# Pacing SyncE's transfers by steps of VectorE, and copying a first product ahead of the exponentials, in a one-core transformer block

## The chip, the cores and the metric

The kernel runs on one core of a Trainium2 chip. The metric is the device time in microseconds (us) of one execution; lower is better. The core has five engines, each with its own queue of instructions that it runs in order: TensorE (PE; PEld is its loading of weights), VectorE (DVE), ScalarE (ACT), GpSimd (POOL) and SyncE (SP). SyncE issues all transfers here; they run on the core's 16 DMA engines. Instructions of different engines wait for each other through semaphores.

## What is computed

16 sequences of 256 tokens with 256 channels go through one block, all in float32:

```
x = x + attention(layernorm(x))      # 16 query heads in 4 groups, 4 key/value heads, 128 wide
x = x + ffn(layernorm(x))            # one 256x256 linear layer, rounded to int8 values
# attention: key s is seen by query t if s <= t and (s < 4 or s >= t - 31)
attn = softmax(q @ k.T / sqrt(128), masked);  out = attn @ v;  return out @ wo.T
# ffn: x and weight are scaled by max|.|/127 per row, rounded, multiplied, scaled back, + bias
```

## The kernel before

**Units and steps.** A unit is one sequence n with one group g of four heads; there are U = 64 units, in the order of `units`. The main loop (`for i in range(U - NT)`) makes 62 steps, one for each of the units 0 to 61; the last two units are written out by hand behind it. Step i computes the scores and the softmax of unit i, the queries of unit i + 1, and parts of the work of older units. Steps 4k to 4k + 3 belong to sequence k.

**Scores.** Queries are taken in blocks of 16 tokens. For each block the keys that it can see (48 in a window and 4 sinks) stand together, so that the scores of a unit are one 128 x 8 x 52 array. `unit_scores` issues TensorE's products into `pss` (L593), VectorE's scaling and masking (L599), the negated row maximum `nmax` (L608), and gives back a function that issues chosen ones of the eight exponentials on ScalarE (L613). `normalised` (L620) divides by the sums, turns the array in 32 x 32 blocks into `z` on VectorE (L627) and stores it as `zd` in DRAM (L629); its inner function `back` reads it again, in four DMAs, as the turned weights `ad` (L638). These `back` functions are kept in `ways[i]`.

**Values.** The values of a sequence are computed for pairs of heads: pair 0 and pair 1. Each takes one chunk of TensorE's work (`start_chunk`; the chunks of sequence n stand at the ends of steps 4n - 3 to 4n, in the order keys 0, values 0, keys 1, values 1). In the step after it, ScalarE copies the products out of PSUM (`both_banks`, L347), GpSimd combines them into `vt`, and `store` writes them as `vd` to DRAM (L536). `values_to` (L457) then reads them into the windows, `vw`: for each half j of the 128 partitions one DMA of 336 KB (L466), one of 16 or 32 KB (L471) and one of 32 KB (L472). There is one `vw` buffer for each pair (`vws`).

**Visits.** In odd steps from 3 on, `times_values` (L675) multiplies the weights `ad` of the units i - 3 and i - 2 with `vw` into `po` (L685). ScalarE copies `po` into `oT` (L696), GpSimd forms sums of it (`left_sums`, L291), and the output projection `py` follows in later steps.

**Queries.** From sequence 1 on, the projections are computed with seven block products in place of eight (Strassen's scheme in Winograd's form). `queries` issues the seven products of two heads into two PSUM banks (`pq`, L89) and returns a `Products`. Its `first` copies the first product to SBUF as `p_q` on ScalarE (L341); `combine` (L326 to L330) makes the two heads' queries `qt` of it in five VectorE operations, whose first one reads that copy. In sequence 0 the products are plain, and one ScalarE copy (L564) takes each over into `qt`. Each step has two such pieces, k = 0 and 1. The pool `ps_m` has four PSUM banks; `pq`, `po`, the chunks' products and others take turns in them.

**What sets the order.** Every engine runs its instructions in the order in which the program writes them (`in_written_order`). Work that belongs to other sequences is hung on a step and a point of it with `at(step, point, f)`, and `do(step, point)` writes it there: loads of x (`load_x`, at "leave" of step 4(n - 1) - 5), statistics (`norm_stats`), the turning of x and of the layer's input through DRAM (`zd_xnT`, `xnT`, `zd_hb`, `hb`; L410 and L419) and the parts of the layer, whose `leave` stores the output. A `back` of an even unit is called at the end of the next step (a visit), that of an odd unit at the start of the step after it; behind the latter, `stores` calls `values_to` for both halves. The lines in question:

```python
        if i - 1 in ways and not visit:
            ways.pop(i - 1)()
            for f in stores:
                f()
            stores = []
...
        for k, q in enumerate(ps):
            exps(range(done, 1 + 3 * k))
            done = 1 + 3 * k
            q.first() if isinstance(q, Products) else q()
        exps(range(done, NK2))
```

So ScalarE's order in a step is: exponential 0, copy for k = 0, exponentials 1 to 3, copy for k = 1, exponentials 4 to 7.

Of the kernel before, what the change touches and what calls it, by code (L numbers as in the profile page):

```python
# [34 lines left out]
def kernel(  # L35
# [11 lines left out]
    nc = tc.nc  # L47
    pe, dve, act, pool, sp = nc.tensor, nc.vector, nc.scalar, nc.gpsimd, nc.sync
    B, T, DM = x.shape
    P = 128  # L50
    D = 128
    H = wqT.shape[1] // D
    G = wkT.shape[1] // D
    HG = H // G
    NC = DM // P
    NT = T // P
# [6 lines left out]
    NJ = 2  # L63
# [33 lines left out]
    def load_x(n):  # L97
        if n < B:
            xts[n] = xp.tile([P, NT, DM], FP, tag="x", name=f"x_{n}")
            sp.dma_start(xts[n], x_v[n])  # L100
# [41 lines left out]
    half = const.tile([P, NT], FP, name="half")  # L142
# [314 lines left out]
    def values_to(n, pair, vd, row):  # L457


        w = vws[pair]  # L460
        vw[n, pair] = w
        base = vd.offset
        for j in range(NJ):
            r = j * HALF
            first = NJ * QB + j * QB - WIN
            sp.dma_start(  # L466
                w[r : r + NW, 1:],
                bass.AP(vd.tensor, base + first * row, [[row, NW], [NJ * QB * row, NK2 - 1], [1, 2 * D]]),
            )
            live = (j + 1) * QB  # L470
            sp.dma_start(w[r + NW - live : r + NW, 0], bass.AP(vd.tensor, base, [[row, live], [1, 2 * D]]))  # L471
            sp.dma_start(  # L472
                w[r + NW : r + NK], bass.AP(vd.tensor, base, [[row, SINK], [0, NK2], [1, 2 * D]])
            )

    def plain_keys(n, pair):
        pk = ps_m.tile([P, 2, T], FP, tag="m", name=f"pk_{n}_{pair}")
# [15 lines left out]
    def plain_values(n):  # L493
        pv = m_banks(f"pv_{n}")
        for t in range(NT):
            for c in range(NC):
                mm(
                    pv[t].rearrange("p k d -> p (k d)"), xnT[n][:, c, t * P : (t + 1) * P], wv_sb[:, c, :],
                    start=(c == 0), stop=(c == NC - 1),
                )  # L500

        def rest():
            vd = dram.tile([T, G * D], FP, tag="vp", name=f"vp_{n}")
            for t in range(NT):
                if t == 0:
                    to = p1.tile([P, 3, 2, D], FP, tag="vt", name=f"vt_{n}_{t}")
                    to = to[:, 0:2].rearrange("p j e d -> p (j e d)")
                else:
                    to = p2.tile([P, HG * T], FP, tag="oT", name=f"vt_{n}_{t}")[:, 0 : G * D]
                act.copy(to, pv[t].rearrange("p k d -> p (k d)"))  # L510
                sp.dma_start(vd[t * P : (t + 1) * P], to)

            def placed(pair):
                values_to(n, pair, vd[:, pair * 2 * D : (pair + 1) * 2 * D], G * D)

            return placed

        return rest
# [9 lines left out]
    def values(n, pair):  # L528
        p = m_banks(f"pv_{n}_{pair}")
        for to, left, right in products(p, factors(n, wv_sb, wv_sums, pair)):  # L530
            mm(to, right, left, start=True, stop=True)
        v = p1.tile([P, 3, 2, D], FP, tag="vt", name=f"vt_{n}_{pair}")

        def store():
            vd = dram.tile([T, 2 * D], FP, tag="vd", name=f"vd_{n}_{pair}")
            sp.dma_start(vd.rearrange("(j p) d -> p j d", p=P), v[:, 0:2].rearrange("p j e d -> p j (e d)"))  # L536
            return lambda: values_to(n, pair, vd, 2 * D)

        return Products(p, f"v_{n}_{pair}", (v[:, 0:3:2, 0], v[:, 2, 1], v[:, 1, 0], v[:, 0:2, 1])), store

# [233 lines left out]
    def by_dma(n):  # L774
        return n < B - 2
# [147 lines left out]
    U = len(units)  # L923
# [2 lines left out]

    POINTS = ("load", "chunk", "gap", "narrow", "early", "turn", "linear", "late", "pool", "leave")
    tasks = {}  # L930

    def at(place, point, f):
        assert point in POINTS
        tasks.setdefault((place, point), []).append(f)

    def do(place, point):
        for f in tasks.pop((place, point), []):
            f()

    chunks = {}  # L940
    for n in range(1, B):
        p = n * G
# [8 lines left out]
    for n in range(2, B):  # L951
        p = (n - 1) * G
        if n > 2:
            at(p - 5, "leave", lambda n=n: load_x(n))
        at(max(p - 4, 1), "early", lambda n=n: norm_stats(n))
        at(p - 2, "early", lambda n=n: norm(n))
        way = []
        at(p - 2, "late", lambda n=n, way=way: way.extend(turned_by_blocks(xns[n], p2, f"xnT_{n}")))
        at(p - 1, "load", lambda way=way: way[0]())
        at(p - 1, "early", lambda n=n, way=way: xnT.__setitem__(n, way[1]()))  # L960
        at(p, "late", lambda n=n: channels(n))
# [10 lines left out]
    for n in range(B - 1):  # L972
        p = n * G + G + 3
        steps = {}

        def step(k, n=n, steps=steps):
            if not steps:
                steps.update(ffn_steps(n))
            steps[k]()

        if by_dma(n):
            plan = (("stats", 1, "early"), ("norm", 2, "early"), ("scale", 2, "late"), ("quantise", 2, "late"),
                    ("clip", 3, "pool"), ("turn", 3, "late"), ("out", 3, "leave"), ("back", 4, "load"),
                    ("narrow", 5, "early"), ("linear", 5, "linear"), ("rest", 7, "early"), ("leave", 8, "leave"))
        else:
            plan = ()
            ffn_last = step
        if n == B - 3:
            ffn_last_but_one = step
            plan = plan[:4]  # L990
        if n == B - 4:
            ffn_last_but_two = step
            plan = plan[:-2]
        for k, after, point in plan:
            at(p + after, point, lambda k=k, step=step: step(k))
# [16 lines left out]
    for f in first_queries:  # L1012
        f()

    ways, waiting, stores, sums = {}, None, [], []
    def start_chunk(i):
        if i == 0:
            return "plain", plain_keys(0, 1)
# [14 lines left out]
    for i in range(U - NT):  # L1033
        visit = i % 2 == 1 and i >= 3
        do(i, "load")
        if i - 1 in ways and not visit:
            ways.pop(i - 1)()
            for f in stores:
                f()
            stores = []  # L1040
        exps, sm = unit_scores(i)
        if i == 0:
            first_values = plain_values(0)
        do(i, "gap")
        kind = waiting and waiting[0]
        if kind == "plain":
            waiting[1]()
        elif kind:
            waiting[3].both_banks()
            waiting[3].combine(pool)  # L1050
        if kind == "v":
            stores.append(waiting[4]())
        for f in sums:
            f()
        sums = []
        do(i, "pool")
        do(i, "turn")
        ps = [queries(*units[i + 1], 0)]
        if i == 0:
            first_values = first_values()  # L1060
            first_values(0)
            at(1, "load", lambda: ways.pop(0)())
            at(1, "load", lambda: first_values(1))
        ps.append(queries(*units[i + 1], 1))
        done = 0
        for k, q in enumerate(ps):
            exps(range(done, 1 + 3 * k))
            done = 1 + 3 * k
            q.first() if isinstance(q, Products) else q()
        exps(range(done, NK2))  # L1070
        for q in ps:
            if isinstance(q, Products):
                q.combine(dve)
        do(i, "early")
        rests = [r for r in (output_part(*o) for o in output_parts(i) if o[0] >= 0) if r]
        for r in rests:
            r[0]()
        values_out = [times_values(u) for u in (i - 3, i - 2)] if visit else []
        for r in rests:
            r[1]()  # L1080
        ways[i] = normalised(i, sm)
        for k, (copied, summed) in enumerate(values_out):
            copied()
            if k == 0:
                summed()
            else:
                sums.append(summed)
        for r in rests:
            r[2]()
        if kind == "k":  # L1090
            keys_to(waiting[1], waiting[2])
        waiting = start_chunk(i)
        if i == U - NT - 1:
            for k in range(2):
                queries(B - 1, G - 1, k, plain=True)()
        do(i, "linear")
        do(i, "late")
        do(i, "leave")
        if i - 1 in ways:
            ways.pop(i - 1)()  # L1100
    assert not tasks and not waiting, sorted(tasks)
    for f in sums:
        f()

    a, b, n = U - 2, U - 1, B - 1
    ways.pop(a - 1)()
    for f in stores:
        f()
    exps_a, sm_a = unit_scores(a)
    exps_b, sm_b = unit_scores(b)  # L1110
    normal_a, turn_a, copied_a = turned_twice(a, sm_a)
# [96 lines left out]
```

## Time and profile before

| what | us |
|---|---|
| three runs | 679.08, 679.09, 682.23 |
| their median | 679.09 |
| the profiled execution | 680.51 |
| its span, first to last instruction | 678.7 |
| DMA packets of queue q1 (SyncE's), MB | 95.34 |
| SyncE's DMAs of values, vw<-vd | 60 of 336 KB, 90 of 32 KB, 30 of 16 KB |
| SyncE's DMAs of weights, ad<-zd | 248 of 64 KB |
| VectorE waiting for the copy p_q (L326 <- L341) | 38.8, in 59 waits |
| ScalarE waiting for nmax (L613 <- L608) | 117.8, in 61 waits |
| VectorE waiting for x (L212) | 13.1, in 10 waits |

Lines of a profile name an engine, a line of the program, an operation and "output<-input" tiles. A row of waits says who waited for whom: total time, number of times, longest. A row of the timeline gives start, duration and, in brackets, how long the engine had been idle before it and what ended that. "Issue" stands for time in which an engine waited for nothing that the profile shows. Windows give the busy time of each engine within a stretch, the granted clock, the mean busy share of the DMA engines and GB/s.

### The profile page before, as it was taken

The numbers are of one execution on the slowest core, as the hardware profiler recorded it, in microseconds if no ns is written. First come the engines' busy times: TensorE is split into PE (matmuls) and PEld (weight loads), VectorE is DVE, ScalarE is ACT, GpSimd is POOL, SyncE is SP. The second block draws the span as 40 slices with busy tenths as digits, with TensorE's granted clock in tenths as the row PEclk, the third lists the DMA queues.
The fourth block names the chain that finished last, engine by engine and source line by source line (L and its number), as shares of the span: only waits on it lengthen the run. The fifth ranks groups of instructions, "written<-read, shape, count | busy, mean of one in ns | idle before, by whom it ended". The sixth has DMA issues, their size and how long they took to land.

```text
span 678.7 us, 35702 instructions
## 1 busy us (share of the span) xinstructions
PE 658.9 (97%) x14956; PEld 623.7 (92%) x14956; DVE 527.0 (78%) x1362; ACT 440.0 (65%) x1626; POOL 527.3 (78%) x823
## 2 busy tenths in 40 slices
PE   9989999999999999999999999999999999999995
PEld 6678899999999999999999999999999999999873
DVE  3757668888788878878788787888869888787775
ACT  3685657657676667667757666766657666665641
POOL 4789578687997868789687887878798787787634
PEclk9999999999999999999999999999999999999998
DMA  8567564566756656666656756556674656656420
GB/s 285 141 169 182 138 146 103 118 163 128 176 138 150 148 117 166 140 155 146 157 130 137 180 139 154 133 118 178 135 178 118 157 140 137 156 128 157 113 67 32
DMA packets 152929, 97.62 MB, mean 144 GB/s; under 512 B 69440, under 2 KB 143040, under 8 KB 152768
## 3 DMA queue, kind: packets, MB, share of 16 engines
q1 hardware_dynamic: 152768, 95.34, 58.4%
q8 instruction: 118, 1.93, 1.3%
q14 instruction: 43, 0.35, 0.2%
HBM read 59.11 MB, written 36.18 MB: 140 GB/s over the span
## 4 chain that ended last, share of the span: by engine, by line
PE 89%; DVE 5%; ACT 2%; issue 2%; DMA 1%; SPq 0%; POOL 0%; DVEq 0%; ACTq 0%
PE py L89 28%; PE pq L89 27%; PE po L685 10%; PE pss L593 8%; PE pk L89 8%; PE pv L89 7%; ACT scores L613 1%; PE pa L89 1%; PE warm L89 1%; DMA vw<-vd 1%; DVE qt L328 0%; ACT qt L564 0%; DVE nmax L608 0%; DVE qt L326 0%; DVE scores L599 0%
## 5 line engine op out<-in xcount | busy, mean ns | idle before, releaser
L613 ACT ACTIVATE scores<-scores,nmax 128x52 f32<-128x52 f32 x512 | 167.9, 332 | 117.8 <-DVE nmax L608 117.8
L89 PE MATMUL pq<-xs,wq_sums 128*64 128x128 f32 x1416 | 122.2, 273 | 0.0
L613 ACT ACTIVATION_READ_ACCUMULATOR scores<-scores,nmax 128x1 f32 x512 | 97.8, 191 | 0.0
L291 POOL TENSOR_TENSOR os<-oT 128x256 f32<-128x256 f32 x56 | 43.8, 781 | 68.8 <-ACT oT L696 68.8
L89 PE MATMUL pq<-xnT,wq_sb 128*64 128x128 f32 (+1 forms) x1104 | 93.9, 290 | 1.5 <-ACT b_v L347 1.5
L89 PEld LDWEIGHTS pq<-xs,wq_sums 128*64 128x64 f32 x1416 | 92.1, 137 | 0.0
L89 PE MATMUL py<-wo_sb,oT 128*64 128x128 f32 (+1 forms) x1152 | 89.7, 297 | 0.0
L696 ACT COPY oT<-po 128x512 f32<-128x512 f32 x124 | 66.4, 588 | 34.5 <-PE po L685 30.5
L685 PEld LDWEIGHTS po<-ad,vw 52*64 52x64 f32 x4096 | 70.8, 134 | 15.8 <-issue 9.6
L89 PE MATMUL py<-wo_sums,os 128*64 128x128 f32 x1344 | 84.6, 273 | 0.0
L685 PE MATMUL po<-ad,vw 52*64 52x64 f32 x4096 | 77.2, 221 | 7.4 <-issue 5.3
L326 DVE TENSOR_TENSOR qt<-pq,p_q 128x256 f32<-128x256 f32 x118 | 49.5, 420 | 38.8 <-ACT p_q L341 38.8
L89 PEld LDWEIGHTS py<-wo_sb,oT 128*64 128x64 f32 x1152 | 70.4, 137 | 8.3 <-issue 0.3
L89 PEld LDWEIGHTS py<-wo_sums,os 128*64 128x64 f32 x1344 | 76.9, 137 | 0.1
L89 PEld LDWEIGHTS pq<-xnT,wq_sb 128*64 128x64 f32 x1104 | 67.6, 137 | 7.3 <-ACT b_v L347 1.7
L593 PE MATMUL pss<-kt,qt 128*64 128x52 f32 x2048 | 72.2, 222 | 0.4 <-ACT qt L564 0.2
L593 PEld LDWEIGHTS pss<-kt,qt 128*64 128x64 f32 x2048 | 70.0, 138 | 2.0 <-ACT qt L564 1.0
L599 DVE SCALAR_TENSOR_TENSOR scores<-pss,masks 128x416 f32<-128x416 f32 x62 | 36.0, 580 | 33.1 <-PE pss L593 33.1
L328 DVE TENSOR_TENSOR qt<-pq,qt 128x256 f32<-128x256 f32 x118 | 50.1, 425 | 13.3 <-PE py L89 0.9
L347 ACT COPY b_v<-pv 128x512 f32<-128x512 f32 (+1 forms) x60 | 31.7, 532 | 42.8 <-PE pv L89 40.7
L89 PE MATMUL pq<-xs,wq_sb 128*64 128x128 f32 x472 | 49.1, 273 | 0.0
L89 PE MATMUL pq<-xnT,wq_sums 128*64 128x128 f32 x472 | 49.1, 273 | 0.0
(192 smaller groups left out, 1622.7 us busy)
## 6 DMA issues: line engine op xcount, KB each, us to landing
vw<-vd SPq DMA_DIRECT2D x60, 336.0 KB
zd<-z SPq DMA_DIRECT2D x62, 256.0 KB
ad<-zd SPq DMA_DIRECT2D x248, 64.0 KB
vd<-vt SPq DMA_DIRECT2D x30, 256.0 KB
x<-in_x_dram SPq DMA_DIRECT2D x15, 256.0 KB
out_dram<-y SPq DMA_DIRECT2D x15, 256.0 KB
zd_xnT<-z_xnT SPq DMA_DIRECT2D x56, 64.0 KB
xnT<-zd_xnT SPq DMA_DIRECT2D x56, 64.0 KB
```

The lines of the kernel that those rows point to most:

```text
L89: pe.matmul(to[c : c + HALF], left[:, c : c + HALF], right, start=start, stop=stop)
L291: pool.tensor_add(s[0], a21, a22)
L326: eng.tensor_add(c11_u, like(p[0][:, 0:2], c11_u), two(p1, c11_u))
L328: eng.tensor_add(c21_c22, like(p[1][:, 0:2], c21_c22), v.unsqueeze(1).to_broadcast(c21_c22.shape))
L347: act.copy(copies[k], self.p[k][:, 0 : 4 - k])
L593: pe.matmul(pss[j * HALF : (j + 1) * HALF, k, :], qt[n, g][:, t, bt].rearrange("p h i -> p (h i)"), kt[n, g // 2][:, g % 2, b, :], start=T ...
L599: dve.scalar_tensor_tensor(s[:, :, 0:NK], pss, SCALE, masks, ALU.mult, ALU.add)
L613: act.activation(s[:, k, 0:NK], s[:, k, 0:NK], AF.Exp, bias=nmax[:, k : k + 1], scale=1.0, accum_out=sm[:, k : k + 1],)
L685: pe.matmul(po[j][d0 : d0 + HALF, k].rearrange("p (a y) -> p a y", a=2), vw[n, g // 2][r, kb, v0 : v0 + HALF], ad[k][r], start=True, stop= ...
L696: act.copy(to[:, j], po[j].rearrange("p k (h i) -> p k h i", i=QB))
```

## The change

`values_to` no longer issues both halves; it returns `half(j)`, which issues the three DMAs of one half. The points of a step are renamed, and three new ones are named after places in VectorE's work. `do_behind(place, point, mark)` writes what hangs on a point and makes the first instruction so written wait for the instruction `mark`, the last one written before: "t2" stands behind `nmax` of the step's scores, "t4" behind the combination of the first queries, "t6" behind that of the second.

- In an even step from 4 on, the weights `ad` of the even unit i - 2 are read at its start, and those of the odd unit i - 1 at "t2".
- Pair 0 of sequence k (combined in step 4k - 1): its first half is read at "t4" of step 4k, its second at "t2" of step 4k + 1. Pair 1 (combined in step 4k + 1): its first half at "t4" of step 4k + 2, its second at "t6" of step 4k + 4.
- `load_x` goes from "leave" to "t6" of the same step, and the output's store from "leave" of one step to "t6" two steps later.
- In ScalarE's order the copy for k = 0 stands ahead of all exponentials, and that for k = 1 behind two of them; the other six follow.

```diff
@@ values_to
-        for j in range(NJ):
+        def half(j):
             r = j * HALF
...
+        return half
@@ values
-            return lambda: values_to(n, pair, vd, 2 * D)
+            return values_to(n, pair, vd, 2 * D)
@@ points
+    written = nc.cur_bb.bb.instructions
+    def do_behind(place, point, mark):
+        k = len(written)
+        do(place, point)
+        if len(written) > k:
+            tc.add_manual_dep(
+                written[k], mark, mybir.DependencyInfo(mybir.DependencyClass.Sync, mybir.DependencyReason.DATA),
+                reason="paced",
+            )
...
-            at(p - 5, "leave", lambda n=n: load_x(n))
+            at(p - 5, "t6", lambda n=n: load_x(n))
...
-                    ("narrow", 5, "early"), ("linear", 5, "linear"), ("rest", 7, "early"), ("leave", 8, "leave"))
+                    ("narrow", 5, "early"), ("linear", 5, "linear"), ("rest", 7, "early"), ("leave", 10, "t6"))
@@ the loop over steps
-        if i - 1 in ways and not visit:
-            ways.pop(i - 1)()
-            for f in stores:
-                f()
-            stores = []
+        if i > 1 and i % 2 == 0:
+            if i > 2:
+                ways.pop(i - 2)()
+            at(i, "t2", ways.pop(i - 1))
         exps, sm = unit_scores(i)
+        do_behind(i, "t2", written[-1].name)
...
         if kind == "v":
-            stores.append(waiting[4]())
+            arrive = waiting[4]()
+            if i % G == 3:
+                at(i + 1, "t4", lambda arrive=arrive: arrive(0))
+                at(i + 2, "t2", lambda arrive=arrive: arrive(1))
+            elif i < U - NT - 1:
+                at(i + 1, "t4", lambda arrive=arrive: arrive(0))
+                at(i + 3, "t6", lambda arrive=arrive: arrive(1))
...
-            exps(range(done, 1 + 3 * k))
-            done = 1 + 3 * k
+            exps(range(done, 2 * k))
+            done = 2 * k
             q.first() if isinstance(q, Products) else q()
         exps(range(done, NK2))
-        for q in ps:
+        for k, q in enumerate(ps):
             if isinstance(q, Products):
                 q.combine(dve)
+            do_behind(i, ("t4", "t6")[k], written[-1].name)
...
-        if i - 1 in ways:
-            ways.pop(i - 1)()
@@ behind the loop
-    ways.pop(a - 1)()
-    for f in stores:
-        f()
+    for i in (a - 2, a - 1):
+        ways.pop(i)()
+    for j in range(NJ):
+        arrive(j)
```

More of the change, by code (lines that the diff above doesn't have):

```diff
@@ L513, in placed @@
             def placed(pair):
-                values_to(n, pair, vd[:, pair * 2 * D : (pair + 1) * 2 * D], G * D)
+                half = values_to(n, pair, vd[:, pair * 2 * D : (pair + 1) * 2 * D], G * D)
+                for j in range(NJ):
+                    half(j)
             return placed
@@ L924 @@
     units[-1] = units[-2]
-    POINTS = ("load", "chunk", "gap", "narrow", "early", "turn", "linear", "late", "pool", "leave")
+    POINTS = ("load", "gap", "pool", "turn", "early", "linear", "late", "leave", "t2", "t4", "t6")
     tasks = {}
@@ L1013 @@
         f()
-    ways, waiting, stores, sums = {}, None, [], []
+    ways, waiting, sums = {}, None, []
     def start_chunk(i):
@@ L1105 @@
     a, b, n = U - 2, U - 1, B - 1
-    ways.pop(a - 1)()
-    for f in stores:
-        f()
+    for i in (a - 2, a - 1):
+        ways.pop(i)()
+    for j in range(NJ):
+        arrive(j)
     exps_a, sm_a = unit_scores(a)
```

## The prediction

> **What bounds the kernel now.** I read the busy table and the chain of the page first, then TensorE's waits in the steady part of the loop, then single steps in the timeline.
>
> ```profile
> PE 658.9 (97%) x14956; PEld 623.7 (92%) x14956; DVE 527.0 (78%) x1362; ACT 440.0 (65%) x1626; POOL 527.3 (78%) x823
> ...
> q8 instruction: 118, 1.93, 1.3%
> ...
> PE 89%; DVE 5%; ACT 2%; issue 2%; DMA 1%; SPq 0%; POOL 0%; DVEq 0%; ACTq 0%
> ```
>
> TensorE is busy for 97% of 678.7 us and is 89% of the chain that ended last; transfers are 1% of it. The change removes no TensorE instruction, so it can win only from what TensorE waits. Its waits between 46 and 637 us (steps 4 to 61) are three groups (columns: total us, times, longest):
>
> ```profile
> PE po L685 <- issue: 5.3, 7, 1.0
> PE po L685 <- DVE qt L330: 1.2, 3, 0.5
> PE pk L89 <- issue: 1.0, 3, 0.6
> ```
>
> That is 7.5 us, 1.1% of the time: the ceiling for the steady loop. No group names a transfer of values or of weights (vw, ad). "Issue" means that no semaphore explains the gap. Queue q8 does: 1.93 MB over TensorE's 29,912 instruction rows is 64 bytes each, in 118 packets of 16 KB, so it is TensorE's instruction stream, one block per 256 rows. At the largest gap one such packet starts at 226.86 us, and TensorE resumes 2.5 us after it. The products with the values (po, 128 small matmuls in 2.1 us) eat one block faster than the next one comes.
>
> Two windows around that gap (columns: window, its length, busy time of each engine, clock, share of the DMA engines, GB/s) show what the fetch shares the engines with:
>
> ```profile
> 222.00:226.50 4.50, 4.50 (x96) 4.33 (x95) 3.50 (x11) 3.70 (x20) 4.05 (x8) 1.00 1.07 185
> 226.50:229.50 3.00, 2.00 (x122) 1.86 (x116) 2.86 (x6) 1.97 (x5) 2.10 (x2) 1.00 0.51 157
> ```
>
> The DMA engines are full (1.07) for 4.5 us before the gap: eight weight pieces, both halves of the values and the next zd pile up. The reader sees TensorE full (4.50 of 4.50) in the crowd and idle for 1.0 of 3.0 us after it.
>
> **The change, part by part.**
>
> *Copies ahead of the exponentials, steady steps.* One step of ScalarE and VectorE today:
>
> ```profile
> 222.80 0.34 ACT L613 ACTIVATE scores<-scores,nmax 128x52 f32<-128x52 f32 x1 [2.13 <-DVE nmax L608]
> 223.05 0.19 ACT L613 ACTIVATION_READ_ACCUMULATOR scores<-scores,nmax 128x1 f32 x1
> 223.14 0.24 ACT L341 COPY p_q<-pq 128x128 f32<-128x128 f32 x1
> ...
> 223.42 0.42 DVE L326 TENSOR_TENSOR qt<-pq,p_q 128x256 f32<-128x256 f32 x1 [0.65 <-ACT p_q L341]
> ```
>
> ScalarE idles 2.13 us for nmax, while the first product of the queries stands in PSUM about 0.3 us after 221.34 (pq's first matmuls). The copy (0.24) moves into that idle time and costs nothing; if the product were late it would delay eight exponentials by 0.24. VectorE's 0.65 us wait goes (38.8 us over 59 steps in the waits), so both combinations end 0.65 us earlier. The second copy goes from behind the fourth exponential to behind the second, and VectorE reaches it only after five operations of the first combination (1.8 us), so it binds nothing. What TensorE gets: the three waits on qt L330, of 0.5 us at most, are below 0.65, so all 1.2 us go. Next late is TensorE itself. **-1.2** (bounds 0 and -1.2).
>
> *The same copies in steps 0 to 2.* There (n = 0) the copy is of the whole plain product, 0.58 us, and it must wait for it. Step 0: ScalarE runs one exponential at 18.46, then waits until 19.70 for the product. With the copy first, two exponentials follow it instead of three before the second copy (which waits until 21.43 in both), and six after it instead of four: 2 x 0.33 = 0.66 us later. In step 1 the product is ready early, so nothing is added. But VectorE's chain behind step 0's exponentials feeds the transposed x and GpSimd's sums, and TensorE already waits 0.16 us for those (pk, 29.36): +0.66 on TensorE. In step 2 the first product is done at 33.8, and its copy ends 0.5 us after the exponentials would have begun (34.05); the second, at 35.75, now holds up six exponentials and not four: +0.6. So ScalarE comes up to 1.28 us later to b_v, and there TensorE waits already:
>
> ```profile
> 41.65 0.66 PE L89 MATMUL pq<-xnT,wq_sb 128*64 128x128 f32 x8 [1.47 <-ACT b_v L347]
> ...
> 44.38 1.22 PE L685 MATMUL po<-ad,vw 52*64 52x64 f32 x64 [0.72 <-DVE qt L330]
> ```
>
> Behind it step 3's combinations gain back about 0.4, since they no longer wait for an exponential; they are what TensorE waits for at 44.38 and 46.09. 1.28 - 0.4 = **+0.85** (bounds +0.2, if step 0's delay stops at VectorE, and +1.3).
>
> *Values in halves, weights and x paced.* Bytes and DMAs stay (804 DMACopy in both programs); their places change, and SyncE's order with them. In a step 4k today SyncE issues x, the output, 8 ad and 6 vw DMAs from 214.49 to 223.5, and only then the next zd (223.60, though z was ready at 221.14). Changed: the even unit's ad at the step's start; the odd unit's behind nmax; the first half of pair 0 behind the first combination; the second half of pair 1 of the sequence before behind the second combination; zd; and pair 0's second half behind nmax of step 4k+1. Step 4k+2 gets one half instead of two. x goes from the end of step 4k+3 into its middle, and the output to the middle of 4k+1. Queued behind each wait on VectorE are vd, zd, hb and xnT of that step; the latest mark (second combination, about 216.0 in step 20) stands well before zd's own release (221.14), so no wait holds them.
>
> Who waits for the pieces: the tightest is pair 1's second half, issued at about 216 in 4k and read by po at 226.25. Three issues take 0.43 + 0.46 + 0.33 us and 336 KB at the window's 185 GB/s 1.8 us: landed at 220 to 222, 4 to 6 us in hand. Cost 0; without that cover every us late would be a TensorE wait in some 14 steps. VectorE's waits for x (13.1 us in 10) go too, but end in no TensorE wait listed above.
>
> *The fetch.* This is the uncertain term. Between 222 and 226.5 the engines moved 185 GB/s x 4.5 = 830 KB; the change leaves there a half of the values with its small pieces, 390 KB, and part of zd and vd. Instruction packets last 0.88 to 0.96 us in quiet stretches, and 1.55, 1.50, 1.60 and 1.53 us at four of the gaps (307.24, 387.94, 469.18, 549.90); three other gaps have 1.08 to 1.17. Without the crowd 4 x 0.65 + 3 x 0.2 = 3.2 us would go by the packets alone. I take 60% of it, **-1.9**, since vd (256 KB at 226.4) stays and the output and x (256 KB each) move close to these gaps. Bounds: all 6.3 us of issue (-6.3), and a crowd that is worse (+5.3: the stalls in po double).
>
> The Trainium skill, DMA: Bandwidth & Descriptors, section "Queues, rings and completion order", says that each DMA engine takes turns between queues packet by packet. By it a crowd delays a fetch by a few packets only, and the fetch term would be near zero; the packet times above differ by 0.65 us, which is more than nothing, but no row here shows the wait ahead of a packet's start.
> The same page, "Rules for kernel authors", calls it useless to split a transfer over partition halves, since both run on the same engines; it would put the halves at 0 in themselves. Here they are spread in time, which no row of before shows.
>
> **Sum.** -1.2 + 0.85 - 1.9 = -2.25. The profiled execution took 680.51 us (span 678.7 and 1.8 around it): 678.3. The median of the three runs, 679.09, is 1.42 below the profiled one: **676.9**. About 0.5%, 3.4 us, is what a measurement of this kernel can tell from no change.
>
> **Rivals.**
> - *TensorE never starves* (20%): the crowd was the whole of the issue waits. 679.09 - 1.2 - 6.3 + 0.85 = 672.4. For it: four of seven gaps have slow packets. Against: the gap at 148.43 (0.60) has a packet of 1.08, and at 226.86 the packet is 1.09 of the 2.5 us until TensorE resumes.
> - *Hidden anyway* (22%): pacing moves transfers that nobody waited for, and the fetch is as late as before: 679.09 - 1.2 + 0.85 = 678.7.
> - *Slower: the new half meets the fetch* (12%): in 4k+1 the second half is issued at about 222.8 to 224 and moves until 226; if vd and the output then close up behind it, the block that po needs comes later in every such step. Doubling the po stalls: 679.09 + 5.3 + 0.85 - 1.2 = 684.0. It decides from some 0.6 us more per gap. The window's share of 1.07 today speaks against it: there is little left to worsen.
> - Something else, such as a piece that lands after po begins: 4%, above 684.
>
> **Chances.** The forecast has 42%, with its own range 675 to 679. Faster by over 0.5% (below 675.7): the first rival and a quarter of the forecast's share, 0.30. Slower (above 682.5): 0.15. Within: 0.55. The range, 672 to 682, reaches from the first rival with the least start cost to the second with the dearest start and some fetch loss; it leaves out the slower ones.
>
> **What the profile will show.** Right: VectorE's wait on p_q near zero; no TensorE wait on qt L330 after 46 us; the DMA share before po in steps 4k+1 under 1.0 and the issue group smaller by a third; TensorE's wait for b_v near 41 us longer than 1.47. Wrong: issue waits that grow or move to steps 4k+3, a TensorE wait on vw or ad, or step 3 as quick as before.

## The result, and the profile after

The changed kernel takes 697.04 us in the median of 6 runs (694.48 to 702.46), against 679.89 us of the kernel before in 6 runs: 1.026 of its time, with a 95% interval of 1.0213 to 1.0307. Forecast were 676.9 us and a range of 672 to 682. The profiled execution's span is 695.6 us, 16.9 more than before.

The page of the changed kernel, busy table and chain:

```profile
PE 663.1 (95%) x14956; PEld 627.5 (90%) x14956; DVE 508.1 (73%) x1362; ACT 451.9 (65%) x1626; POOL 527.9 (76%) x823
...
PE 76%; DMA 9%; DVE 7%; SPq 2%; issue 2%; ACT 1%; POOL 1%; DVEq 0%; POOLq 0%
```

The instructions are the same, but transfers have gone from 1% to 9% of the chain that ended last. TensorE's waits between 46 and 637 us (total, times, longest) name them:

```profile
PE po L690 <- DMA vw<-vd: 13.6, 8, 2.7
PE pk L89 <- issue: 3.8, 5, 1.1
PE po L690 <- DVE z L632: 3.0, 2, 1.5
```

Neither the first nor the third row was there before. (po stands at L690 in the changed file, at L685 before.) In the third row VectorE had long been done; the wait stands at the same place as the first.

Where in the loop the time went follows from the scores in the two traces; the start of a step is taken here as the middle of TensorE's products for them. From the first scores to the last, the changed kernel takes 16 us more (641.1 against 625.1). The steps 4k + 1 from 9 to 57 take 150.2 us together, 133.0 before: all of the loss and 1.2 more. The steps 4k + 3 from 7 to 59 take 138.2 against 140.0, steps 0 to 3 0.9 more. In a step 4k + 1, po multiplies the weights with pair 1 of the values, and where it waits, it stops after its first four matmuls; the fifth is the first that reads the second half.

Not all of the 16.9 us is idle time. TensorE idles 12.7 us more (32.5 against 19.8), and for the same instructions it is busy 4.2 us longer (663.1 against 658.9). Its granted clock is 0.988 of full speed over the execution, 0.997 before. Up to step 61 the trace has three spells of 3.41 us at half clock, from 44.22, 150.04 and 276.33, and the kernel before has none there. The last two begin 0.7 and 1.3 us after po resumed from waits for values in steps 13 and 25. Windows over the wait in step 13 and over the spell behind it:

```profile
146.67:149.37 2.70, 0.01 (x1) 0.04 (x1) 2.53 (x7) 1.23 (x4) 1.49 (x2) 1.00 1.15 225
150.05:153.45 3.40, 3.40 (x104) 3.28 (x95) 0.00 (x0) 2.13 (x4) 1.56 (x3) 0.50 0.46 148
```

Over the six runs the granted clock is 0.983 to 0.993. The waits of 2.38 and 2.37 us in steps 21 and 37 have no such spell behind them, so the trace does not say when one comes.

How late the second half is can be read in SyncE's timeline of step 20, which starts at 215.2 (start, duration, what):

```profile
215.13 0.56 SPq L541 DMA_DIRECT2D vd<-vt  x1
216.13 0.41 SPq L100 DMA_DIRECT2D x<-in_x_dram  x1
216.65 3.36 SPq L419 DMA_DIRECT2D xnT<-zd_xnT  x4
220.11 0.56 SPq L634 DMA_DIRECT2D zd<-z  x1
220.77 4.38 SPq L643 DMA_DIRECT2D ad<-zd  x8
225.25 0.38 SPq L467 DMA_DIRECT2D vw<-vd  x1
...
226.60 0.30 SPq L467 DMA_DIRECT2D vw<-vd  x1
...
227.45 0.32 SPq L473 DMA_DIRECT2D vw<-vd  x1
227.88 0.34 SPq L634 DMA_DIRECT2D zd<-z  x1
228.32 0.38 SPq L467 DMA_DIRECT2D vw<-vd  x1
```

When the step starts, SyncE still works on step 19: its vd, x and turned x. The next zd, whose z was ready at 214.5, goes out at 220.11, the eight weight pieces take until 225.15, and pair 1's second half (226.60 to 227.77) follows the first half of pair 0. Its mark, the second combination, had ended at 220.6 and held nothing. In step 21, po starts at 230.90. The chain over this stretch shows the rest:

```profile
227.45 6.03 DMA vw<-vd
233.48 0.14 issue
233.62 2.16 PE po L690 x124
```

The last of the three transfers lands 6.03 us after its issue. Over the steps 13 to 57 that wait (eleven; in step 17 for only 0.3 us), the last of these three issues stands 9.5 to 12.8 us behind the start of step 4k, TensorE resumes 4.8 to 7.1 us after it, and po is due at 15.7. In steps 9, 33 and 61 the issue comes at 6.7 to 9.0 us, and there is no wait. So the half has to be issued by about 9 us into step 4k, and it mostly is not.

### The profile page after: what moved, and what is told of

Read it like the earlier page. It is cut to its first block, busy times and chain, and to the rows that moved or that the text cites. A ratio compares the mean times of both kernels' runs of the same rounds, so it can differ in the third digit from the quotient of the medians.

```text
span 695.6 us, 35837 instructions
## 1 busy us (share of the span) xinstructions
PE 663.1 (95%) x14956; PEld 627.5 (90%) x14956; DVE 508.1 (73%) x1362; ACT 451.9 (65%) x1626; POOL 527.9 (76%) x823
## 4 chain that ended last, share of the span: by engine, by line
PE 76%; DMA 9%; DVE 7%; SPq 2%; issue 2%; ACT 1%; POOL 1%; DVEq 0%; POOLq 0%
PE py L89 22%; PE pq L89 21%; PE po L690 10%; PE pk L89 8%; PE pss L598 8%; DMA vw<-vd 7%; PE pv L89 6%; DMA zd<-z 2%; DVE scores L604 1%; SPq L472 1%; DVE nmax L613 1%; DVE qt L326 1%; SPq L643 1%; DVE qt L328 1%; SPq L467 1%
## 5 line engine op out<-in xcount | busy, mean ns | idle before, releaser
L291 POOL TENSOR_TENSOR os<-oT 128x256 f32<-128x256 f32 x56 | 45.6, 814 | 82.2 <-ACT oT L701 82.2
L341 ACT COPY p_q<-pq 128x128 f32<-128x128 f32 x118 | 31.4, 266 | 108.3 <-PE pq L89 108.3
L690 PEld LDWEIGHTS po<-ad,vw 52*64 52x64 f32 x4096 | 72.7, 139 | 25.1 <-issue 19.2
L690 PE MATMUL po<-ad,vw 52*64 52x64 f32 x4096 | 78.9, 226 | 16.9 <-DMA vw<-vd 13.6
```

The lines of the kernel that those rows point to most:

```text
L291: pool.tensor_add(s[0], a21, a22)
L341: act.copy(self.p1, region(self.p, 1))
L690: pe.matmul(po[j][d0 : d0 + HALF, k].rearrange("p (a y) -> p a y", a=2), vw[n, g // 2][r, kb, v0 : v0 + HALF], ad[k][r], start=True, stop= ...
```

## The experiments

Theory A: pair 1's second half is too late, since its place in SyncE's queue puts its issue some 4 us ahead of po. Rival B: the added waits on VectorE hold SyncE, and all comes late. Rival C: ScalarE's new order costs it.

**Pair 1's half early** (e1):

```diff
-                at(i + 3, "t6", lambda arrive=arrive: arrive(1))
+                at(i + 1, "t6", lambda arrive=arrive: arrive(1))
```

> The changed kernel with one place moved: the second half of pair 1 is read in step 4k + 2, behind the second combination (right behind its first half), and not two steps later in step 4k + 4. Theory A (that half is issued by SyncE about 4 us before the products po of step 4k + 1 read it, and lands after they begin): TensorE's 13.6 us of waits on vw<-vd go, steps 4k + 1 come back from 11 to 14 us to 9.7 to 10.9, the time is 676 to 681. Rival B (the waits on VectorE hold SyncE back, and all that it issues comes late): little changes, 690 or more. Rival C (the copies ahead of the exponentials cost it): unchanged, 695 to 699.

676.05 us in the median, 0.9944 of the kernel before (0.9923 to 0.9965). Its TensorE waits between 46 and 637 us:

```profile
PE po L690 <- issue: 2.0, 3, 0.8
PE pk L89 <- issue: 0.2, 1, 0.2
PE pss L598 <- ACT qt L569: 0.2, 1, 0.2
```

No wait names a transfer, and the issue waits are 2.2 us, not the 6.3 of the kernel before (e12 shows how far this number scatters). One moved line turns +2.6% into -0.6%: A, and not C.

**Without the added waits** (e2): the `add_manual_dep` of `do_behind` is taken out; order and places stay.

```diff
-        if len(written) > k:
-            tc.add_manual_dep(
...
-            )
```

> The changed kernel with the same order of SyncE's transfers, but without the added waits on VectorE's instructions. Theory A (place of pair 1's second half in SyncE's queue, behind eight weight pieces and pair 0's half): SyncE comes to it 1 us earlier at most, so most of the loss stays, 688 to 697. Rival B (the added waits hold SyncE): back to 677 to 681. Rival C: unchanged.

696.19 us, 1.0211 (1.0167 to 1.0255). Most of the loss stays without any pacing wait, so B falls.

**The copies alone** (e3), put into the kernel before:

```diff
-            exps(range(done, 1 + 3 * k))
-            done = 1 + 3 * k
+            exps(range(done, 2 * k))
+            done = 2 * k
```

> The kernel before with ScalarE's new order alone: a copy ahead of the exponentials, two exponentials, the second copy, six exponentials. Theory A: what the prediction gave the copies, -1.2 us in the steady steps and +0.85 in steps 0 to 3: 0.997 to 1.003 of before. Rival C: 1.02 or more.

679.43 us, 1.0004 (0.998 to 1.0028): C falls. VectorE's wait for p_q is 0.8 us, from 38.8, and TensorE's wait on qt behind step 4 is 0.5, from 1.2. At the start the wait for b_v, 1.47 us before, has grown as forecast:

```profile
43.03 0.66 PE L89 MATMUL pq<-xnT,wq_sb 128*64 128x128 f32 x8 [2.10 <-ACT b_v L347]
```

Steps 0 to 3 take 0.5 us more than before.

**The pacing alone** (e4): the changed kernel with the same two lines turned back.

> The changed kernel with ScalarE's old order (exponential, copy, three exponentials, copy, four exponentials). Theory A: the loss stays, 1.02 to 1.03 of before, TensorE's waits on vw<-vd remain 10 us or more, and VectorE's wait on p_q is 38 us again. Rival C: 0.997 to 1.003.

701.63 us, 1.0302 (1.027 to 1.0333). The waits on vw<-vd that the profile names are 8.9 us, a little less than expected, but four more rows of po waits (9.4 us together) stand behind vd, sm, scores and qt; all but 0.5 us of these are in steps 4k + 1 as well. VectorE's wait for p_q is 38.8 us again. The loss is that of the transfers.

**Pair 1's half in the same step, but ahead of the weights** (e5):

```diff
-                at(i + 3, "t6", lambda arrive=arrive: arrive(1))
+                at(i + 3, "load", lambda arrive=arrive: arrive(1))
```

> The changed kernel with pair 1's second half at the very start of step 4k + 4, ahead of the eight weight pieces in SyncE's queue and without a wait on VectorE; it is read in the next step as before. Theory A1 (it is issued late, because it stands behind eight weight pieces of 4.4 us of issuing and pair 0's first half of 1.2 us): it lands some 5 us earlier, the waits on vw<-vd go, 677 to 682. Theory A2 (it is the landing that is slow, 6 us behind the issue, whatever the place): waits of 5 us or more stay and the time is 685 or more.

680.72 us, 0.997 (0.9949 to 0.9991). SyncE's timeline of step 20, which starts at 211.5 here:

```profile
215.72 0.55 SPq L634 DMA_DIRECT2D zd<-z  x1
216.31 0.43 SPq L467 DMA_DIRECT2D vw<-vd  x1
...
217.34 0.33 SPq L473 DMA_DIRECT2D vw<-vd  x1
217.77 0.31 SPq L643 DMA_DIRECT2D ad<-zd  x1
```

The half goes out 4.8 to 5.8 us into the step, not 11.4 to 12.3, and no step waits for it, though po reads it in the same place as in the changed kernel. The place in the queue is the cause. The issue waits are 7.3 us here and 2.2 in e1, but the two ratios cannot be told apart.

**Pair 0's half out of its way** (e6):

```diff
-                at(i + 2, "t2", lambda arrive=arrive: arrive(1))
+                at(i + 2, "t6", lambda arrive=arrive: arrive(1))
```

> The changed kernel with pair 0's second half read behind the second combination of step 4k + 1 and not behind nmax, so that it does not follow pair 1's late half within 1 us. Pair 1's half keeps its late place. Theory A1 (late issue alone): unchanged, 693 to 699. Theory A2 (what is issued behind it shares the DMA engines and draws out its landing): the wait of po shrinks by half or more, 682 to 690.

695.59 us, 1.0178 (1.0142 to 1.0213): above what the sharing of the engines would have given, a little below the changed kernel. But the time hides two opposite movements. Of TensorE's waits, in a profile of the longest of the six runs (701.47):

```profile
PE po L690 <- DMA vw<-vd: 7.1, 6, 1.8
PE pk L89 <- issue: 4.4, 5, 1.2
PE pss L598 <- issue: 3.5, 3, 2.2
```

The wait of po for the half is 7.1 us; in the changed kernel it was 13.6, or 16.6 with the row that names z. It shrank by more than half, as A2 had it. The issue waits grew from 3.8 to 10.4 us, and that took most of the gain. Part of the gain is the landing: where the last of the three issues stood 11.3 to 12.4 us into step 4k, TensorE resumed 5.0 to 6.1 us after it, 6.0 to 6.4 in the changed kernel. So what is issued behind the late half seems to draw out its landing by some 0.7 us (5.5 and 6.2 in the mean); how much of the loss that makes, this run does not settle. The late issue itself remains in both kernels.

**Early, without the added waits** (e7): the edits of e1 and e2 together.

> The kernel e1_pair1_early without the added waits on VectorE, its order of transfers kept. If the order of SyncE's queue does what e1 gained: 0.993 to 0.997 of before, like e1. If the waits do it (they keep the DMA engines from filling ahead of po, so that TensorE's instructions come in time): 0.998 to 1.003, and TensorE's issue waits are back at 5 to 6 us from 2.2.

676.15 us, 0.9905 (0.9875 to 0.9934), with issue waits of 2.9 us. The order of SyncE's queue does it; the waits on VectorE add nothing that shows.

**Early, both halves together** (e8): e1 with

```diff
-                at(i + 2, "t2", lambda arrive=arrive: arrive(1))
+                at(i + 1, "t4", lambda arrive=arrive: arrive(1))
...
-                at(i + 1, "t6", lambda arrive=arrive: arrive(1))
+                at(i + 1, "t4", lambda arrive=arrive: arrive(1))
```

> The kernel e1_pair1_early with both halves of a pair read together: pair 0 behind the first combination of step 4k, pair 1 behind that of step 4k + 2. If arriving in halves is worth something of its own (less crowd ahead of po in steps 4k + 1): 0.997 to 1.002 of before and issue waits of 4 us or more. If not: like e1, 0.992 to 0.996.

679.9 us, 0.9959 (0.9936 to 0.9983). The ratio does not tell it from e1. The issue waits are 7.9 us, in a profile of the longest of its runs (684.37), and lean to the halves without showing it:

```profile
PE po L690 <- issue: 5.3, 5, 1.5
PE pk L89 <- issue: 1.8, 4, 0.8
```

**The old order of ScalarE where the products are plain** (e9: e7 with it; e12: the same with the added waits):

```diff
-            exps(range(done, 2 * k))
-            done = 2 * k
+            ready = 2 * k if isinstance(q, Products) else 1 + 3 * k
+            exps(range(done, ready))
+            done = ready
```

> The kernel e7_early_no_marks (pair 1's second half in step 4k + 2, no added waits) with ScalarE's old order kept in steps 0 to 2, where the copy is of a whole plain product, and the new order from step 3 on. TensorE's wait for b_v near 42 us falls from 2.1 to 1.5 us and its waits for xs near 29 us from 0.6 to 0.2: 0.5 to 1 us below e7 if the prediction's start term is right; no change if it is not. 0.989 to 0.994 of before.

> The kernel e9_best_no_marks with the added waits on VectorE, to compare the waits on one chip. If the waits as such are worth nothing, as e7 against e1 has it: the same as e9 within 0.3%. If they pace: faster than e9 by 0.3% or more.

677.34 us, 0.993 (0.9907 to 0.9954), and 677.63 us, 0.9935 (0.991 to 0.996). The wait for b_v is back at 1.46 us in both and that for xs at 0.15. The half microsecond itself is too small for these intervals. The added waits are worth nothing on one chip either. e12 differs from e1 by ScalarE's order in steps 0 to 2 alone, and still its issue waits are 5.7 us (1.4 of them at the end of step 3) and not 2.2. So this number seems to scatter by 2 to 3 us between single profiles, and a smaller difference between two kernels says nothing.

**x and the output at their old places** (e10): e7 with the two moves turned back.

```diff
-            at(p - 5, "t6", lambda n=n: load_x(n))
+            at(p - 5, "leave", lambda n=n: load_x(n))
...
-                    ("narrow", 5, "early"), ("linear", 5, "linear"), ("rest", 7, "early"), ("leave", 10, "t6"))
+                    ("narrow", 5, "early"), ("linear", 5, "linear"), ("rest", 7, "early"), ("leave", 8, "leave"))
```

> The kernel e7_early_no_marks with the loads of x and the stores of the output at their old places (ends of steps). If these two moves carry part of the gain: 0.994 to 1.0 of before and VectorE waits for x of 10 us or more, with TensorE waiting 2 us more. If the order of weights and values carries it: like e7, 0.988 to 0.994, whatever VectorE waits for x.

679.42 us, 0.9967 (0.9948 to 0.9987), on the chip on which e9 had 0.993. VectorE waits 27.4 us for x, 2.2 in e9. TensorE's waits behind other engines are not 2 us longer. The two intervals touch, and e9 also has the old order in steps 0 to 2. From e7, which differs by the two moves alone, the interval stands apart (0.9875 to 0.9934), but e7 ran on another chip. So a part in the gain is likely and not shown.

**The instruction stream shifted** (e11), in the kernel before:

```diff
         mm(warm, ones, ones, start=True, stop=True)
+    for _ in range(10):
+        mm(warm[:, 0:32], ones, ones[:, 0:32], start=True, stop=True)
```

> The kernel before with 20 small matmuls (32 columns) more behind the warm-up at its start: 80 rows of TensorE's instruction stream, nothing else. If the issue waits in po come from the instruction stream's blocks of 256 rows, the block borders fall 80 rows (40 matmuls) earlier in every po: the gaps in steps 13, 21, 29, 37, 45 (behind 95 to 119 matmuls) go, and gaps come in steps 15, 23, 31, 39, 47, where the border lay behind the end of po. If they come from the transfers of steps 8k + 5, they stay in those steps. The time: 0.998 to 1.003 of before.

686.62 us, 1.007 (1.0039 to 1.0102), slower than expected. Half of the forecast of the gaps came true. The issue gaps behind 95 to 119 matmuls of po in steps 13, 21, 29, 37 and 45 are gone (steps 21, 29 and 45 have shorter ones, 0.2 to 0.5 us, at the first or the fifth matmul); the new late ones are not in steps 15 to 47 but in 41 and 49, behind 122 and 116 matmuls:

```profile
438.24 0.34 PE L685 MATMUL po<-ad,vw 52*64 52x64 f32 x6 [0.60 <-issue]
...
519.66 0.45 PE L685 MATMUL po<-ad,vw 52*64 52x64 f32 x12 [0.97 <-issue]
```

The shares of the DMA engines, worked out from the trace's packets (2.5 us ahead of po to 0.5 us into it) go with this: 1.07 and 1.01 in steps 41 and 49, and 0.43 to 0.56 in steps 15, 23, 31, 39 and 47. In the kernel before five of the seven gaps in po stood in steps with 1.05 to 1.12, one (step 53) at 0.93; the seventh, step 55, at 0.58 is not told by the share. So a border late in po does not seem to be enough; most of these gaps stand where the engines are full too. The largest issue wait of this run, 1.8 us, is elsewhere, at the scores of step 6. Of the time, 1.3 us is the longer start; in steps 21, 29, 37 and 45 TensorE waited for VectorE (qt, sm), which waited 26.2 us for x in all (13.1 before), and the clock stood at half for 3.41 us from 231.78. Why x came later was not tried.

**Quiet engines ahead of po** (e13): e9 with the edit of e6.

> The kernel e9_best_no_marks with pair 0's second half behind the second combination of step 4k + 1 and not behind nmax, so that the DMA engines are emptier in the 2.5 us ahead of po (share 0.95 in the kernel before in steps 8k + 5, 0.78 in e9_best_no_marks). If TensorE's issue waits come from its instruction blocks meeting full DMA engines: share under 0.5 there, issue waits at most 2 us from 4.1, 0.5 to 2 us below e9, 0.986 to 0.992 of before. If the crowd does not matter: 0.991 to 0.996 and issue waits of 4 us.

679.2 us, 0.9935 (0.9909 to 0.9961). Windows ahead of po in step 21 and behind it (length, engines, clock, DMA share, GB/s):

```profile
224.20:227.20 3.00, 3.00 (x82) 2.83 (x81) 2.75 (x10) 2.76 (x15) 2.68 (x5) 1.00 0.33 88
228.00:232.00 4.00, 4.00 (x130) 3.93 (x131) 3.86 (x7) 3.18 (x7) 3.79 (x5) 1.00 0.98 264
```

and TensorE's issue waits:

```profile
PE pk L89 <- issue: 2.7, 4, 1.6
PE po L690 <- issue: 1.2, 2, 0.9
PE pss L598 <- issue: 1.1, 3, 0.5
PE pq L89 <- issue: 1.0, 2, 0.7
```

The share ahead of po is 0.21 in the mean of steps 8k + 5. All of the steps 13 to 53 there take 9.67 to 9.75 us, which is what they take without a gap (up to 10.9 before). In e9 three of these six steps have a gap and in the kernel before all six, so that part of the theory holds. But the whole gained nothing that shows over e9, which ran on another chip: the crowd stands behind po now (0.98 from 228 to 232), and 4.8 us of the 6.0 are in pk, pss and pq, 3.5 of them right behind the po of steps 4k + 1. The gap seems to move with the crowd.

Over all runs (issue waits of TensorE from 46 to 637 us in one profile each; share as above, mean of the steps 8k + 5):

| kernel | ratio | issue waits, us | share ahead of po |
|---|---|---|---|
| before | 1 | 6.3 | 0.95 |
| changed | 1.026 | 3.8 | 1.01 |
| e1 early | 0.9944 | 2.2 | 0.72 |
| e2 changed, no waits | 1.0211 | 6.8 | 0.88 |
| e3 copies alone | 1.0004 | 5.0 | 0.92 |
| e4 pacing alone | 1.0302 | 4.3 | 1.03 |
| e5 ahead of the weights | 0.997 | 7.3 | 0.94 |
| e6 pair 0 later | 1.0178 | 10.4 | 0.58 |
| e7 early, no waits | 0.9905 | 2.9 | 0.70 |
| e8 early, whole | 0.9959 | 7.9 | 0.78 |
| e9 | 0.993 | 4.1 | 0.78 |
| e10 x and output back | 0.9967 | 4.5 | 0.74 |
| e11 stream shifted | 1.007 | 5.0 | 0.79 |
| e12 | 0.9935 | 5.7 | 0.81 |
| e13 quiet ahead of po | 0.9935 | 6.0 | 0.21 |

The intervals of e1, e5, e7, e8, e9, e10, e12 and e13 all lie below 1. Those of e1, e7, e9, e12 and e13 overlap and do not rank them. The share ahead of po does not order the issue waits over kernels: e6 and e13 have the lowest shares and not the lowest waits. The granted clock of the profiled executions is 0.982 to 0.988 in the changed kernel, e2, e4 and e6, the four with the late half, and 0.993 to 0.997 in all others.

## Why the prediction was wrong

**The step that failed** is the one that cost the pacing at 0: "the tightest is pair 1's second half, issued at about 216 in 4k", "landed at 220 to 222, 4 to 6 us in hand". It took the mark's time for the time of issue. The mark is only the earliest time; SyncE comes to the transfer after everything ahead of it in its queue. The prediction had the row: SyncE was still issuing from 214.49 to 223.5 in a step that began at 210.5. Step 20 of the changed kernel issues the half 11.4 us into the step, not 5.5, and e5, which differs only in the place in the queue, has no such wait.

The same step gave the landing 1.8 us, bytes over the window's 185 GB/s. The last piece took 6.03 us. With the issue at 216 that alone would still have been in time; the two errors together were not.

Its own price for the case was right: "every us late would be a TensorE wait in some 14 steps". Steps 4k + 1 lost 17.3 us in 13 steps, 1.3 us each. The price left out the clock: waits this long had spells at half clock behind them in two steps, some 1.7 us each (half of 3.41). The case was put at 4%, beside a priced slower rival (the new half meets the fetch, 684 us) that is not what happened.

**The copies in the steady steps** (-1.2) were right in kind: in the changed kernel no wait on qt is left behind step 4, and in e3 0.5 of 1.2 us. **The copies in steps 0 to 2** (+0.85, bounds 0.2 to 1.3) came out at 0.5 us in e3 and 0.9 us in the changed kernel, whose clock was at half for 3.41 us from 44.22 on, as e3's was not. The waits grew at the places named: xs near 29 us and b_v near 42. Together the copies are 1.0004 of before in e3.

**The fetch** (-1.9): the issue waits did fall, from 6.3 to 3.8 us, but not for the reason given. The share ahead of po in steps 8k + 5 did not fall; it went from 0.95 to 1.01, since the late half, zd and pair 0's half still meet there. The six gaps in po of those steps are gone, but in all six po now stands for its values instead, so this is no gain. In e1, where the share is 0.72, 4.1 of the 6.3 us went, but in e12, which differs from it in steps 0 to 2 alone, only 0.6 (2 without the wait at the end of step 3); what the order is worth to the fetch stays open. The way that the prediction priced it, by the length of the instruction packets, does not hold: those of 16 KB last 1.17 us in the mean before and 1.20 in e1. What moved is their start. Against the start of po in steps 21, 29 and 37 it went from +0.61, -0.02 and -0.19 us before to -0.66, -0.65 and -0.86 in e1; in step 45, where it did not move (-0.24 and -0.27), e1 still has a gap. The Trainium skill's rule in DMA: Bandwidth & Descriptors, "Queues, rings and completion order", that engines take turns between queues packet by packet, would have made a crowd nearly harmless for a fetch; e13's steps 8k + 5 without a gap and e11's new gaps in po, both in full steps, speak against that use of it, whatever the engines' turns are.

**VectorE's waits for x** went from 13.1 to 2.3 us, as expected. That they "end in no TensorE wait" is left in doubt by e10.

## What to carry to other kernels

The time of a transfer on a shared queue is the later of its mark and its place: add up the issues that stand ahead of it, with the durations that the queue's own timeline shows, and start from when the queue really finishes the step before. A deadline then needs the landing measured among the neighbours that it will have, which was 6 us here for what bytes over bandwidth made 1.8. In this kernel, whose TensorE is 97% busy, the orders with that transfer early took 0.3 to 1% off, for reasons that are only partly shown; the same transfer too near its reader cost 2.6%, part of it not as waiting but as TensorE running at half clock behind the longest waits.

## What the runs showed of the hardware

TensorE's instruction stream comes in packets of 16 KB over the same DMA engines, and it seems to run dry for up to 1.8 us (e11). In the kernel before, this came mostly where a block's border falls late in a run of small matmuls (128 in 2.1 us) while the DMA engines are full: e11 moved the gaps by shifting the stream, e13 took them out of one place by emptying the engines there. After long waits TensorE's clock can stand at half for 3.41 us: two such spells behind waits of 2.70 and 1.69 us in the changed kernel. Issue from SyncE is itself dear: eight weight pieces of 64 KB took 4.38 us in the changed kernel and 5.17 in e5.
